# When ScalarE scales an expert's result rows: behind the copy of U3, or behind the silu of C12

## The chip, the core and the metric

The kernel runs on one core of one Trainium2 chip. The metric is device time in microseconds (us). Five engines work side by side, each in its own order: TensorE (PE in the profile; its weight loads are PEld), VectorE (DVE), ScalarE (ACT), GpSimd (POOL), and SyncE (SP), which issues DMAs. An engine's instruction waits on semaphores that other engines raise, and everything queued behind it on that engine waits with it.

## The reference, cut to what matters

The model block is a gated cross-attention followed by a gated mixture of experts. Only the second part is touched. Each of 8 experts takes the 615 tokens with the highest claim on it, runs a two-layer network on them, scales each result row by that token's gate, and adds the row to the token's output:

```python
        xg = x[disp_tok].reshape(E, cap, Dm)
        h = jax.nn.silu(jnp.einsum('ecd,edh->ech', xg, W1) + b1[:, None, :])
        out = jnp.einsum('ech,ehd->ecd', h, W2) + b2[:, None, :]
        gated = out * disp_g.reshape(E, cap, 1)
        y = jnp.zeros((N, Dm), x.dtype).at[disp_tok].add(gated.reshape(E * cap, Dm))
```

E is 8, cap is 615 (held as 616 columns, two halves of CH = 308), Dm is 512, and the hidden width is 2048.

## The kernel before

The attention takes about the first half of the time. After it, the experts run one after another, experts 0 to 7. The order on every engine is the order in which the Python code issues the instructions: both halves stand under `tc.manual_schedule()`, so no planner moves anything.

An expert has an up projection in NP = 8 steps, `up(e, i, hook)` for i = 0 to 7, and then a down projection in two parts, `down(e, m, hook)`. One step of `up` makes two blocks of 128 hidden units for both halves of the columns, by Strassen's scheme in Winograd's form: seven products in place of eight. All are fp32 and go through `product` (L933), four matmuls to a product in the profile. In the order of TensorE they are:

1. `p1`, then `p2` (both `ps<-xg_t,w`). ScalarE copies `p1` out to `p1s` (L961); VectorE adds `p2` to it, which gives `c11` (L964); ScalarE takes the silu of it with bias (L957).
2. A product added onto `p1` (`ps<-tg,s1w`). It may start only when `p1s` has been copied out. ScalarE copies the sum to `u2` (L986). Then the product `p5` (also `ps<-tg,s1w`). VectorE forms V = `p5` + `u2` (L991).
3. A product added onto `p1` (`ps<-xg_t,w`); ScalarE copies it to `u3` (L994). VectorE forms `c22` = `p5` + `u3` (L996), ScalarE its silu.
4. The product `p3` (`ps<-xg_t,s1w`); VectorE forms `c12` = `p3` + V (L1001), ScalarE its silu.
5. A last product added onto `p1` (`ps<-tg,w`); ScalarE takes the silu of it directly: silu 21 (L957).

In between, `up` calls `hook(1)` (behind the silu of `c11`) and `hook(3)` (behind the silu of `c12`). The function behind them, `in_up(i, n)`, puts the side work there:

- At `hook(1)`: on VectorE the four sums `sum_h` of the step before (L914 to L917, through `sums_t`), on GpSimd the four weight sums `sum_w1` of the step after (L645 to L648, through `sums_of`), on SyncE the load of a weight block (L656), and `lay_out(e - 1, i)`. The last takes one tile of 128 columns of the *previous* expert's result `o_t`, transposes it in blocks on VectorE (L866 or L870), and issues four DMAs on SyncE (L874) that bring it into rows, in the tile `eo`.
- At `hook(3)`, for i = 1 to 5: `put_laid(e - 1, i - 1)`. It scales the rows that the step before laid out by their gates, on ScalarE and in place (L893), and then issues the scatter that adds them to the output, an indirect DMA from GpSimd (L1101). Expert 0 has no previous expert, so there are 7 x 5 = 35 scalings of this kind; the last expert's rows go another way, after the loops.
- Also at `hook(3)`: `route_on()`, one piece of the selection of tokens for a later expert. A typical piece is `narrow`: one small matmul that counts (L714), and ten small VectorE instructions (L700 to L732).

GpSimd takes its work in the order issued too: the scatter of a step, then the weight sums that `hook(1)` of the next step asks for. Three `eo` tiles and two `s1w` tiles are in use in turn.

In `down` the products are longer (16 matmuls), ScalarE has little to do, and neither scalings nor scatters of `put_laid` are issued.

## Time and profile before

| What | Value |
|---|---|
| median of 3 runs | 2031.45 us (2030.32 to 2032.4) |
| the profiled execution, its time | 2030.15 us |
| the profiled execution, its span in the trace | 2028.4 us |
| granted TensorE clock, mean over the span | 0.977 |
| busy, share of the span: PE, DVE, ACT, POOL | 95%, 63%, 42%, 30% |
| up steps of expert 1: PE busy in 1173 to 1233 us | 59.16 of 60.00 us |
| L893, the scaling | 35 times, median 706 ns |
| L1101, the scatter from `eo` with `slots` | 35 times, median 1560 ns |

Times in the views run from the span's start. In a timeline each row has the start, the time, the engine, the line, the operation, the tiles, and in square brackets the idle time of the engine before it with what ended it; a row marked x4 holds four instructions in a run. A matmul's record reaches a little past the start of the next one, so the spacing of starts is the better measure of PE's pace than the recorded time. One up step without anything else takes 7.26 us in this trace (from one L994 to the next: 1178.59, then 7.26 and again 7.26 later).

### The profile page before, as it was taken

Reading aid. Unit: us, or ns where it says so; the run is one execution under the profiler, and the core shown is the slowest. Engines: PE = TensorE matmul, PEld = TensorE weight load, DVE = VectorE, ACT = ScalarE, POOL = GpSimd, SP = SyncE. Lnnn points to the kernel's source line nnn. Section 1 sums busy time; section 2 is a strip of 40 time slices with the busy share of each in tenths; the row PEclk is TensorE's granted clock in tenths of the full one; section 3 lists DMA queues with packets and bytes.
Section 4 is the critical chain, followed back from the end, with each engine's and each line's share of the span. In section 5 each row is a group of like instructions: output and inputs, shape, how many; then the busy total and the mean of one; then the engine's idle time right before and its main releaser. Section 6 shows DMA issues by size and latency. Waiting matters only on the chain.

```text
span 2028.4 us, 27201 instructions
## 1 busy us (share of the span) xinstructions
PE 1930.5 (95%) x8784; PEld 1151.1 (57%) x8784; DVE 1279.6 (63%) x2693; ACT 851.8 (42%) x2014; POOL 603.5 (30%) x798
## 2 busy tenths in 40 slices
PE   7989999999999999998669999999999999999997
PEld 3334444444444444444346777777777777777775
DVE  3566666667666666766568675776767667772540
ACT  3656667566666756565213032230403223041321
POOL 1001110010111001110135463536545365464533
PEclk9999999999999999998779999999999999999998
DMA  7243434434343443333511545344553534455332
GB/s 259 74 116 90 128 110 120 125 94 139 104 123 110 121 124 96 103 114 89 150 51 52 157 88 135 89 114 117 110 148 87 138 89 111 124 113 136 88 68 26
DMA packets 291678, 224.58 MB, mean 111 GB/s; under 512 B 26768, under 2 KB 260944, under 8 KB 291536
## 3 DMA queue, kind: packets, MB, share of 16 engines
q1 hardware_dynamic: 282704, 201.96, 35.7%
q0 software_dynamic: 8832, 20.88, 5.6%
q8 instruction: 71, 1.16, 0.3%
q14 instruction: 71, 0.58, 0.1%
HBM read 107.75 MB, written 29.77 MB: 68 GB/s over the span
## 4 chain that ended last, share of the span: by engine, by line
PE 73%; DVE 8%; ACT 7%; DMA 4%; issue 4%; SPq 2%; POOL 1%; POOLq 0%; ACTq 0%; DVEq 0%
PE ps L933 40%; PE pj L300 13%; PE po L423 6%; PE s L352 6%; PE pt L236 5%; ACT by_part L375 3%; DVE nm L361 2%; ACT pr L375 2%; DMA laid_p<-by_part 2%; DVE p_t L405 1%; DMA w<-in_W 1%; SPq L874 1%; SPq L380 1%; DVE ht L917 1%; ACT q_t L309 1%
## 5 line engine op out<-in xcount | busy, mean ns | idle before, releaser
L361 DVE TENSOR_REDUCE nm<-s 128x2 f32<-128x1024 f32 x256 | 298.1, 1204 | 52.6 <-PE s L352 52.5
L395 ACT COPY p_t<-pt 128x512 f32<-128x512 f32 x256 | 138.1, 589 | 276.7 <-PE pt L236 276.5
L933 PE MATMUL ps<-xg_t,w 128*128 128x308 f32 x768 | 220.1, 423 | 0.5 <-ACT u L986 0.5
L223 POOL TENSOR_TENSOR rstd<-rstd,nhalf 128x1 f32<-128x1 f32 x64 | 37.0, 578 | 613.9 <-DVE rstd L222 613.9
L352 PE MATMUL s<-k_t,q_t 32*128 32x512 f32 x1024 | 193.9, 653 | 25.4 <-ACT by_part L375 17.8
L933 PE MATMUL ps<-h,w 128*128 128x308 f32 x768 | 207.5, 425 | 0.0
L375 ACT ACTIVATE by_part<-s,nm 128x512 f32<-128x512 f32 x256 | 174.5, 691 | 53.1 <-DVE nm L361 47.8
L933 PEld LDWEIGHTS ps<-xg_t,w 128*128 128x128 f32 x768 | 145.8, 190 | 53.9 <-ACT u L986 1.0
L375 ACT ACTIVATE pr<-s,nm 128x512 f32<-128x512 f32 x256 | 174.4, 697 | 0.0
L933 PEld LDWEIGHTS ps<-h,w 128*128 128x128 f32 x768 | 143.7, 190 | 52.6 <-issue 3.2
L236 PEld LDWEIGHTS pt<-ident,pr 128*128 128x128 f32 x1024 | 112.5, 143 | 103.4 <-issue 100.3
L405 DVE STREAM_TRANSPOSE p_t<-laid_p 128x512 f32<-128x512 f32 x256 | 165.9, 686 | 5.0 <-DMA laid_p<-by_part 4.7
L933 PE MATMUL ps<-tg,s1w 128*128 128x308 f32 x512 | 145.3, 426 | 9.3 <-ACT p1s L961 5.5
L442 DVE TENSOR_TENSOR o_t<-po,over 128x512 f32<-128x512 f32 x32 | 22.1, 691 | 207.3 <-ACT over L438 207.3
L236 PE MATMUL pt<-ident,pr 128*128 128x128 f32 x1024 | 143.4, 284 | 2.7 <-ACT pr L375 2.7
L423 PE MATMUL po<-p_t,v_s 128*32 128x512 f32 x1024 | 142.4, 628 | 0.9 <-DVE p_t L405 0.9
L933 PE MATMUL ps<-ht,s2w 128*128 128x308 f32 x512 | 137.9, 426 | 0.0
L957 ACT ACTIVATE h<-c,b 128x308 f32<-128x308 f32 x192 | 101.4, 549 | 74.3 <-DVE c L996 72.1
L933 PEld LDWEIGHTS ps<-tg,s1w 128*128 128x128 f32 x512 | 94.9, 190 | 52.8 <-issue 20.5
L300 PE MATMUL pj<-ctx_t,wk 128*128 128x512 f32 x256 | 117.0, 600 | 7.1 <-DMA ctx_t<-in_ctx_t 7.1
L933 PEld LDWEIGHTS ps<-ht,s2w 128*128 128x128 f32 x512 | 95.5, 190 | 34.8 <-issue 1.8
L300 PE MATMUL pj<-xn_t,wq 128*128 128x512 f32 x248 | 111.6, 592 | 0.0
(191 smaller groups left out, 3105.0 us busy)
## 6 DMA issues: line engine op xcount, KB each, us to landing
laid_p<-by_part SPq DMA_DIRECT2D x512, 128.0 KB
w<-in_W SPq DMA_DIRECT2D x128, 256.0 KB
w<-in_W SPq DMA_DIRECT2D x64, 512.0 KB
x<-in_x SPq DMA_DIRECT2D x64, 256.0 KB
laid<-xg SPq DMA_DIRECT2D x140, 64.0 KB
out_x<-x SPq DMA_DIRECT2D x32, 256.0 KB
xn_rows<-xn SPq DMA_DIRECT2D x32, 256.0 KB
ctx_t<-in_ctx_t SPq DMA_DIRECT2D x28, 256.0 KB
```

The lines of the kernel that those rows point to most:

```text
L223: nc.gpsimd.tensor_tensor(rstd, rstd, nhalf, ALU.pow)
L236: nc.tensor.transpose(pt[:, c, :], src[:, c * P : (c + 1) * P], ident)
L300: nc.tensor.matmul(ps, lhsT=lhs(ic), rhs=rhs(ic), start=(ic == 0), stop=(ic == DC - 1))
L352: nc.tensor.matmul(ps[i // 2][:, i % 2, :], lhsT=q_t[b, c][r, cols(qc)], rhs=k_t[b, c][r, :], start=True, stop=True,)
L361: nc.vector.tensor_reduce(nm[:, 2 * i : 2 * i + 2], ps[i], AX.X, ALU.max, negate=True)
L375: nc.scalar.activation(to, of, AF.Exp, bias=nm[:, i : i + 1], accum_out=sums[b, c][:, qc, i : i + 1])
L395: nc.scalar.copy(p_t[b, c][i][:, :, cols(qc)].rearrange("p c (q j) -> p c q j", q=DC), pt.rearrange("p c (j q) -> p c q j", q=DC),)
L405: nc.vector.transpose(p_t[b, c][i][:, :, cols(qc)].rearrange("p c (q j) -> p q c j", q=DC), laid[:, :, i - 2].rearrange("p q (c i) -> p q ...
L423: nc.tensor.matmul(po[i * HD : (i + 1) * HD, :], lhsT=v_s[b][:, kc, h * HD : (h + 1) * HD], rhs=pts[i][:, kc, :], start=(kc == 0), stop=(k ...
L442: nc.vector.tensor_tensor(o_t[b][:, c, :], po, over, ALU.mult)
L933: nc.tensor.matmul(ps, lhsT=lhs[k], rhs=rhs[k], start=(k == 0 and not onto), stop=(k == n - 1), skip_group_check=onto,)
L957: nc.scalar.activation(hh[q, i], src, AF.Silu, bias=b1[:, j : j + 1])
```

## The change

`up` gets one more call, `hook(2)`, behind the copy of `u3` on ScalarE and ahead of the sum `c22`. `in_up` puts `put_laid` there and leaves `route_on` at `hook(3)`. Nothing is added or taken away; on ScalarE the scaling now stands ahead of two silus (of `c22` and of `c12`) that it stood behind.

```diff
@@ up
         product([w[:, k, 1, :] for k in k0], [x[:, k, rhalf] for k in k0], p1)
         u3 = temp("u3")
         nc.scalar.copy(u3, p1)
+        hook(2)
         c22 = temp("c", 3)
         tt(c22, p5, u3, ALU.add)
         silu("22", 1, c22)
@@ in_up
             def in_up(i, n):
-
-                if n == 3:
+                if n == 2:
                     if e and 0 < i <= NST:
                         put_laid(e - 1, i - 1)
+                    return
+
+                if n == 3:
                     if e == 0 or i > 1:
                         route_on()
                     return
```

The order of instructions changes on ScalarE alone. On TensorE, VectorE, GpSimd and SyncE every instruction keeps its place and what it waits for.

## The prediction

> **What bounds the kernel now.** I read the page first, then who PE waited for in the stretch of the expert steps (1173 to 2010 us), then the timelines of PE, ScalarE, VectorE and GpSimd for expert 1.

> The page says that TensorE is busy nearly all the time, so only its idle time can be won:

> ```profile
> span 2028.4 us, 27201 instructions
> PE 1930.5 (95%) x8784; PEld 1151.1 (57%) x8784; DVE 1279.6 (63%) x2693; ACT 851.8 (42%) x2014; POOL 603.5 (30%) x798
> ```

> The waits of PE from 1173 to 2010 us (total in us, times, longest) are few, 21 in all:

> ```profile
> PE ps L933 <- issue: 3.0, 12, 0.3
> PE ps L933 <- ACT p1s L961: 2.6, 7, 0.5
> PE ps L933 <- ACT h L957: 0.8, 2, 0.4
> ```

> 21 is 3 for each of the 7 experts that scale rows. The timeline of PE shows where: at the first product that is added onto p1. The first three rows are a step without a stall, the last three one with:

> ```profile
> 1187.66 2.24 PE L933 MATMUL ps<-xg_t,w 128*128 128x308 f32 x8
> 1189.74 2.24 PE L933 MATMUL ps<-tg,s1w 128*128 128x308 f32 x8
> 1191.81 1.20 PE L933 MATMUL ps<-xg_t,w 128*128 128x308 f32 x4
> ...
> 1195.03 2.24 PE L933 MATMUL ps<-xg_t,w 128*128 128x308 f32 x8
> 1197.56 2.31 PE L933 MATMUL ps<-tg,s1w 128*128 128x308 f32 x8 [0.28 <-issue]
> 1199.70 1.20 PE L933 MATMUL ps<-xg_t,w 128*128 128x308 f32 x4
> ```

> The distance of starts is 2.08 us without a stall and 2.53 with one, and the next distance is 2.14 in place of 2.07: a stall shown as 0.28 costs 0.52 us. In expert 1 the other two (at 1205.35 and 1213.32) cost 0.43 and 0.60. They follow steps i = 2, 3 and 4; no stall follows i = 1 and i = 5, though they scale too.

> What PE waits for is p1s, whatever the label: it starts 0.15 us after p1s ends. The timeline of ScalarE:

> ```profile
> 1193.10 0.41 ACT L994 COPY u<-ps 128x308 f32<-128x308 f32 x1 [1.21 <-PE ps L933]
> 1195.10 0.99 ACT L957 ACTIVATE h<-c,b 128x308 f32<-128x308 f32 x2 [1.58 <-DVE c L996]
> 1196.00 0.71 ACT L893 ACTIVATE eo<-eo,gates 128x512 f32<-128x512 f32 x1
> 1196.61 0.50 ACT L957 ACTIVATE h<-ps,b 128x308 f32<-128x308 f32 x1
> 1197.01 0.40 ACT L961 COPY p1s<-ps 128x308 f32<-128x308 f32 x1
> ```

> ScalarE is idle for 1.58 us until c22 comes, and then runs five instructions without a gap; the scaling is in the middle and holds back silu 21 and p1s by 0.61 us (1196.61 less 1196.00). p1 itself was there at about 1196.2. So these steps turn on a loop: p1s, c11, the sums of VectorE, c22, two silus, the scaling, silu 21, the next p1s. c22 is late because VectorE and GpSimd slow each other: the same sum takes 0.47 us in the step where GpSimd rests and 1.00 beside it:

> ```profile
> 1184.05 0.47 DVE L916 TENSOR_TENSOR h<-h,h 128x308 f32<-128x308 f32 x1
> ...
> 1191.78 1.00 DVE L916 TENSOR_TENSOR h<-h,h 128x308 f32<-128x308 f32 x1
> 1192.40 0.96 POOL L647 TENSOR_TENSOR w<-w 128x256 f32<-128x256 f32 x1
> ...
> 1196.98 1.56 POOL L1101 DMA_INDIRECT out_x<-eo,slots  x1 [2.71 <-DMA eo<-laid]
> ```

> The last row shows GpSimd waiting, until 0.27 us after the scaling's end (1196.71): the wait named is an older DMA, the scaling is what came last.

> **The change, part by part.**

> *The scaling leaves the place ahead of p1s.* Per stalled step ScalarE's chain from c22 to p1s is shorter by 0.61 us. PE's lateness at that product (start distances 2.53, 2.43, 2.60 against 2.08) is 0.45, 0.35 and 0.52: each less than 0.61. So each stall goes. Over 21 stalls: 6.4 us shown, plus 0.24 each that the idle time does not show (0.17 of the overlap of two matmuls, 0.07 at the restart), 5.0 us: 11.4 us. Checked by expert 1: 0.52 + 0.43 + 0.60 = 1.55, times 7 is 10.9; experts 5 and 7 have somewhat longer ones. After that the step goes at PE's own pace, 7.26 us, or 7.37 with one counting matmul.

> *The scaling's new place costs nothing.* It stands behind u3 and would run from 1193.5 to 1194.2, in an idle time of 1.58 us (1.49 and 1.66 in the two steps after, 0.89 at i = 5). At i = 1 the idle time is only 0.55, so the silu of c22 comes 0.06 us later; there p1s waits for PE and nothing is lost. Without this cover the price would be 0.61 x 35 = 21 us, if ScalarE were full; it is not.

> *A wait moves forward with it.* The scaling also waits for the four DMAs that bring the rows in. If they are late, the silus of c22 and c12, silu 21 and p1s are queued behind them, and PE behind p1s. The trace's packets of these DMAs: issued from 1185.56, ended by 1189.33; the next sets ended by 1198.12, 1206.19 and 1214.91. The new places of the scalings that use them are about 1193.5, 1200.9, 1208.3 and 1215.7 at PE's new pace, and VectorE's transposes that start the later sets come earlier as well (below). The margins are 4.2, 2.8, 2.1 us, and over 0.8 us at i = 5 even if the transpose did not move. I put nothing.

> *The scatter and, behind it in GpSimd's order, the weight sums move forward.* The scatter starts 0.28 after the scaling, at 1194.5 in place of 1196.98; the sums (1.04 us later) at 1195.5 in place of 1198.0. No instruction of GpSimd waited for PE there, and the `s1w` tile that the sums write is free once PE has passed p3 (1194.1). The scatter's transfer is far from the next one (7 us). What changes is what the sums meet on VectorE: less of L914 to L917, more of `narrow`. In the first such step the sums would start at 1188.3, where VectorE is idle until c11 at 1190.0: `sum_h` is then slowed only in its first half, and c22 comes about 1 us sooner. This is a gain in slack, not counted in us.

> [...] VectorE's load in a full step, from c11 (1197.44) to the end of `narrow` (1205.07), is 7.63 us. `sum_h` takes 3.57 in it (1197.84 to 1201.41) and 1.68 without GpSimd (1183.15 to 1184.83), so undisturbed the load is 5.74. How much will GpSimd add at the new place? The trace has a row near: in `down`, GpSimd's sums meet `narrow`.

> ```profile
> 1195.56 0.17 DVE L718 TENSOR_TENSOR ahead<-ahead,thr 128x7 int32<-128x7 int32 x1
> 1196.23 0.56 DVE L700 TENSOR_TENSOR mask<-gate,cand 128x224 bf16<-128x224 f32 x1
> ...
> 1260.27 0.65 DVE L718 TENSOR_TENSOR ahead<-ahead,thr 128x7 int32<-128x7 int32 x1
> 1261.64 0.97 DVE L700 TENSOR_TENSOR mask<-gate,cand 128x224 bf16<-128x224 f32 x1
> ```

> With L726 (0.38 for 0.17) `narrow` grows by 1.1 us at most. The part of it that GpSimd would meet from 1195.5 on, L726 and L700, grows by 0.6; then L914 and L915 by 0.8 (their rows beside GpSimd), perhaps L916 by 0.5. Sum 1.4 to 1.9, load 7.1 to 7.6, against PE's 7.37. [...] I take the rows: 1.4 to 1.9. Even 7.63 would slip only 0.26 per step for three steps, 0.8 us, inside the 1 us won in the first.

> *Sum:* 2030.15 for the profiled execution less 11.4 is 2018.75. That execution lies 1.3 us under the median, 2031.45; on the median's scale the forecast is 2020.1.

> **The rivals.**

> *VectorE becomes the bound and keeps part of the stalls.* If GpSimd slows VectorE as before and no slack is won, VectorE's chain from 1190.0 to 1210.5 shortens only by its two idle gaps (0.16 and 0.19), and p1s by these and 0.61: 0.96 us per expert in place of 1.55. Expert 7 has no routing and gains all, about 1.8: 6 x 0.96 + 1.8 = 7.5, time 2023.9. For it: VectorE's full steps are without gaps. Against it: GpSimd's sums start 2.5 us earlier, where c11 to c12 read PSUM or VectorE idles.

> *Nothing measurable.* The stalls are there for another reason, such as p1's own lateness: 2031.5. Against it: p1s starts exactly when silu 21 lets it, and in step i = 1, where c22 was early, the same scaling cost PE nothing.

> [...]

> **How the numbers follow.** All stalls gone, 2018.3 to 2022: 0.70. A part kept, 2022 to 2027.4: 0.16. Within 0.2% (4 us, about what a measurement of this kernel can tell from no change): 0.05. Slower: 0.09. The range, 2018.3 to 2026.0, takes the first and nearly all of the second; its lower end is the full gain and the 1.1 to 1.3 us by which runs lie under the median, plus a little.

> **What would show it right or wrong.** Right: no wait of PE at `ps<-tg,s1w` from 1173 to 2010; L893 right behind L994, 2.5 us ahead of before; GpSimd's wait ahead of L1101 shorter; the first L916 of a scaling step back to 0.5; steps of 7.26 or 7.37 in all. Part kept: PE waits at i = 3 and 4 of experts 1 to 6 with VectorE gapless from L964 to L732. Wrong: an idle time of ScalarE ahead of L893 put down to a DMA, L700 and L718 over 1 us, or p1s still 0.15 us ahead of a late PE.

## The result, and the profile after

The changed kernel takes 2022.64 us (median of 5 runs, 2020.46 to 2024.9) against 2031.45 us (5 runs, 2029.3 to 2032.54); the ratio of all runs is 0.9958 with a 95% interval of 0.9943 to 0.9972. A second series beside the experiments gave 2018.81 us (2016.34 to 2020.05) against 2030.33 us: 0.9936, 0.9918 to 0.9954. So the change saves about 9 to 11.5 us. The profiled execution took 2020.52 us. The page after:

```profile
span 2018.7 us, 27201 instructions
PE 1927.6 (95%) x8784; PEld 1153.8 (57%) x8784; DVE 1269.9 (63%) x2693; ACT 857.5 (42%) x2014; POOL 593.4 (29%) x798
```

PE's busy share shows nothing of it, and its waits show all. From 1173 to 2000 us no wait of PE is listed any more, where 21 were listed before. From 1060 us on there are only these, all in expert 0, which scales no rows:

```profile
PE ps L933 <- ACT p1s L961: 2.8, 2, 2.5
PE cnt_ps L714 <- DVE cnt L708: 1.2, 2, 0.8
```

PE's timeline of the two steps of expert 1 that were shown of before:

```profile
1187.92 2.24 PE L933 MATMUL ps<-xg_t,w 128*128 128x308 f32 x8
1190.00 2.24 PE L933 MATMUL ps<-tg,s1w 128*128 128x308 f32 x8
1192.07 1.20 PE L933 MATMUL ps<-xg_t,w 128*128 128x308 f32 x4
...
1195.29 2.24 PE L933 MATMUL ps<-xg_t,w 128*128 128x308 f32 x8
1197.37 2.24 PE L933 MATMUL ps<-tg,s1w 128*128 128x308 f32 x8
1199.44 1.20 PE L933 MATMUL ps<-xg_t,w 128*128 128x308 f32 x4
```

The second step now has the spacing of the first: 2.08 and 2.07 us, where it was 2.53 and 2.14. ScalarE in that step:

```profile
1193.36 0.42 ACT L994 COPY u<-ps 128x308 f32<-128x308 f32 x1 [1.21 <-PE ps L933]
1193.67 0.72 ACT L893 ACTIVATE eo<-eo,gates 128x512 f32<-128x512 f32 x1
1194.75 0.99 ACT L957 ACTIVATE h<-c,b 128x308 f32<-128x308 f32 x2 [0.36 <-DVE c L997]
1195.65 0.50 ACT L957 ACTIVATE h<-ps,b 128x308 f32<-128x308 f32 x1
1196.58 0.42 ACT L961 COPY p1s<-ps 128x308 f32<-128x308 f32 x1 [0.43 <-PE ps L933]
```

The scaling sits in the idle time behind u3, and the copy p1s waits for PE (0.43 us), no longer PE for it. But VectorE and GpSimd in the same step look less calm than the forecast had them (their timelines, one beneath the other):

```profile
1195.04 0.74 DVE L717 TENSOR_SCALAR ahead<-steps 128x7 int32<-128x7 int32 x1
1195.72 1.27 POOL L645 TENSOR_TENSOR s1w<-w 128x256 f32<-128x256 f32 x1
1195.81 1.22 DVE L718 TENSOR_TENSOR ahead<-ahead,thr 128x7 int32<-128x7 int32 x1
...
1199.30 0.47 DVE L964 TENSOR_TENSOR c<-ps,p1s 128x308 f32<-128x308 f32 x1
1200.58 0.47 DVE L916 TENSOR_TENSOR h<-h,h 128x308 f32<-128x308 f32 x1
```

The sums of h are fast again (L916 at 0.47), because in this step GpSimd's weight sums fall on the routing piece `narrow`; there L718 takes 1.22 us in place of 0.17, and c11 comes 4.0 us behind the step's first product (1199.30 less 1195.29), where it came 2.4 behind it before (1197.44 less 1195.03).

Where the 9.7 us between the two spans lie, by the starts of the copies of u3: the stretch from expert 1's first to expert 7's last went from 772.65 to 762.34 us, 10.3 less. The time ahead of expert 0 is 1.4 less, expert 0 takes 1.65 more, the tail 0.4 more. The last three do not come from where the scaling stands: the code there is the same, and other profiles scatter there too (last section). I call the first the *expert stretch* and use it for the experiments, since it repeats to 0.1 us: a second profile of the changed kernel has 762.31. The stalls account for all of it. Added up over the up steps of experts 1 to 7, PE's starts at the product added onto p1, and at the restart behind it, lie 11.38 us too far apart in the profile of before and 1.07 in that of after; the difference is 10.3.

### The profile page after: what moved, and what is told of

Read it like the earlier page. It is cut to its first block, busy times and chain, and to the rows that moved or that the text cites. A ratio compares the mean times of both kernels' runs of the same rounds, so it can differ in the third digit from the quotient of the medians.

```text
span 2018.7 us, 27201 instructions
## 1 busy us (share of the span) xinstructions
PE 1927.6 (95%) x8784; PEld 1153.8 (57%) x8784; DVE 1269.9 (63%) x2693; ACT 857.5 (42%) x2014; POOL 593.4 (29%) x798
## 4 chain that ended last, share of the span: by engine, by line
PE 78%; DVE 7%; ACT 7%; issue 3%; DMA 3%; SPq 2%; POOL 1%; POOLq 0%; ACTq 0%; DVEq 0%
PE ps L933 45%; PE pj L300 13%; PE po L423 6%; PE s L352 6%; PE pt L236 5%; ACT by_part L375 3%; DVE nm L361 2%; ACT pr L375 2%; DMA laid_p<-by_part 2%; DVE p_t L405 2%; SPq L380 1%; ACT q_t L309 1%; PE pj_o L300 1%; DVE mask L700 1%; PE idle L1138 0%
## 5 line engine op out<-in xcount | busy, mean ns | idle before, releaser
L933 PE MATMUL ps<-xg_t,w 128*128 128x308 f32 x768 | 220.7, 423 | 0.5 <-ACT u L986 0.5
L933 PE MATMUL ps<-h,w 128*128 128x308 f32 x768 | 207.5, 425 | 0.0
L933 PEld LDWEIGHTS ps<-xg_t,w 128*128 128x128 f32 x768 | 146.3, 191 | 54.3 <-ACT u L986 1.0
L933 PEld LDWEIGHTS ps<-h,w 128*128 128x128 f32 x768 | 143.7, 190 | 52.6 <-issue 3.2
L933 PE MATMUL ps<-tg,s1w 128*128 128x308 f32 x512 | 145.3, 427 | 3.1 <-ACT p1s L961 2.8
L933 PE MATMUL ps<-ht,s2w 128*128 128x308 f32 x512 | 137.9, 426 | 0.0
L957 ACT ACTIVATE h<-c,b 128x308 f32<-128x308 f32 x192 | 102.3, 550 | 49.1 <-DVE c L997 39.1
L933 PEld LDWEIGHTS ps<-tg,s1w 128*128 128x128 f32 x512 | 96.6, 190 | 41.6 <-issue 5.6
L933 PEld LDWEIGHTS ps<-ht,s2w 128*128 128x128 f32 x512 | 95.5, 190 | 34.8 <-issue 1.8
L352 PEld LDWEIGHTS s<-k_t,q_t 32*128 32x128 f32 x1024 | 53.3, 186 | 102.8 <-ACT pr L375 43.7
```

What stands on the lines that cost most here:

```text
L352: nc.tensor.matmul(ps[i // 2][:, i % 2, :], lhsT=q_t[b, c][r, cols(qc)], rhs=k_t[b, c][r, :], start=True, stop=True,)
L933: nc.tensor.matmul(ps, lhsT=lhs[k], rhs=rhs[k], start=(k == 0 and not onto), stop=(k == n - 1), skip_group_check=onto,)
L957: nc.scalar.activation(hh[q, i], src, AF.Silu, bias=b1[:, j : j + 1])
```

## The experiments

Two explanations were open. A: it is enough that the scaling leaves the place ahead of p1s on ScalarE. B: that alone leaves VectorE as the bound, and what also counts is that GpSimd's scatter and weight sums start earlier and meet other work on VectorE.

**The changed kernel again** (e1). No edit.

> The changed kernel once more, beside the others on one chip. Both theories: 2020 to 2025 us, 6 to 11 us under the kernel before; PE's waits at ps<-tg,s1w in experts 1 to 7 under 0.7 us in total (6.4 before). Where the time lies in this band is open: the profile of the changed kernel had a half-clock window of TensorE of 3.4 us at expert 0's last step, which the profile of before did not have, so runs should differ by steps of about 1.7 us.

Measured: 2018.81 us, 1.2 us under the range I had given; expert stretch 762.3. PE's only listed wait in experts 1 to 7 is one of 0.2 us, as expected.

**The scaling moved, GpSimd held back** (e2).

```diff
@@ in_up, against the changed kernel
                 if n == 2:
                     if e and 0 < i <= NST:
-                        put_laid(e - 1, i - 1)
+                        scale_laid(e - 1, i - 1)      # L893 alone
                     return
                 if n == 3:
+                    if e and 0 < i <= NST:
+                        # GpSimd copies h["12", i][:, 0:1], then the scatter
+                        put_laid(e - 1, i - 1, h[e]["12", i])
```

> The scaling at its new place on ScalarE, but GpSimd held as it was: the scatter is issued at the old place, behind a read by GpSimd of one column of the silu of C12, so that scatter and weight sums start near their old times. Theory A (the 0.61 us that the scaling took between c22 and p1s is enough by itself): PE's waits at ps<-tg,s1w in experts 1 to 7 under 1.5 us, time within 2 us of the changed kernel. Theory B (VectorE is then the bound; the earlier weight sums of GpSimd were needed too): about 0.6 us of loss stays per expert 1 to 6, 3 to 4 us in all, mostly behind steps 3 and 4, and the time is 3 to 4 us above the changed kernel.

Measured: 2025.11 us (2022.78 to 2032.82), ratio to the kernel before 0.997 (0.9957 to 0.9983); expert stretch 767.3. PE's waits in experts 1 to 7, and ScalarE and PE around steps 2 and 4 of expert 1:

```profile
PE ps L939 <- ACT p1s L967: 2.9, 9, 0.5
...
1203.16 0.99 ACT L963 ACTIVATE h<-c,b 128x308 f32<-128x308 f32 x2 [1.03 <-DVE c L1003]
1204.46 0.40 ACT L967 COPY p1s<-ps 128x308 f32<-128x308 f32 x1
...
1219.00 0.99 ACT L963 ACTIVATE h<-c,b 128x308 f32<-128x308 f32 x2 [1.68 <-DVE c L1003]
1220.30 0.40 ACT L967 COPY p1s<-ps 128x308 f32<-128x308 f32 x1
1220.84 2.31 PE L939 MATMUL ps<-tg,s1w 128*128 128x308 f32 x8 [0.39 <-ACT p1s L967]
```

The first of the three stalls is gone. Then c22 comes later from step to step (ScalarE waits 1.03, then 1.68 us for it), and although no scaling stands in the chain, p1s is late and PE stalls. B is right, and by more than I had put on it: the time is 6.3 us above the changed kernel's, where I had 3 to 4.

**The read by itself** (e5), the control to e2.

```diff
@@ put_laid, against the kernel before
         nc.scalar.activation(eo[:m, :], eo[:m, :], AF.Copy, scale=gates[e][:m, s : s + 1])
+        seen = ex.tile([P, 1], F32, tag="seen", name="seen", bufs=2)
+        nc.gpsimd.tensor_copy(seen, behind_h[:, 0:1])     # h[e]["12", i]
```

> The control of e2_scatter_back: the scaling at its old place, and GpSimd's read of the silu of C12 ahead of the scatter. It isolates what the read itself costs, so that the distance to e2 is the scaling's place on ScalarE alone, with GpSimd at about the same times. If the read is harmless: the stretch from expert 1's first copy of u3 to expert 7's last within 1 us of the kernel before (772.7 us in its profile), 21 stalls. If the read itself is what kept part of the loss in e2: that stretch 2 us or more longer than before.

Measured: 2034.81 us against 2031.25, ratio 1.0019 (1.001 to 1.0028); expert stretch 775.8, so 3.1 longer than before. PE's waits in experts 1 to 7, all at the same product under three labels, are still 21, now up to 0.9 us each:

```profile
PE ps L935 <- ACT p1s L963: 8.1, 17, 0.9
PE ps L935 <- issue: 0.9, 3, 0.3
PE ps L935 <- ACT h L959: 0.4, 1, 0.4
```

The read is not harmless: GpSimd's weight sums start 0.2 to 0.3 us later behind u3 than before (means of each step over experts 1 to 7), and the loop pays for it. So e2 must be compared with e5: 775.8 less 767.3, 8.5 us, is about what the scaling's place on ScalarE is worth with GpSimd late. GpSimd does not run at the very same times in both: in e2 the scatter starts 0.1 to 0.2 us earlier behind u3 in steps 1 and 2, and 0.2 to 0.6 us later in steps 3 to 5. The remaining 6.1 us, down to the 761.2 of a loop without stalls (e3, next), are what a late GpSimd costs, the read included.

**The weight sums early, the scaling at its old place** (e3).

```diff
@@ in_up, against the kernel before
                 if n == 3:
                     if e and 0 < i <= NST:
+                        if i + 2 < NP:
+                            sum_w1(e, i + 2)
                         put_laid(e - 1, i - 1)
...
-                if 0 < i < NP - 1:
+                if 0 < i < NP - 1 and not (e and 1 < i <= NST + 1):
                     sum_w1(e, i + 1)
```

> The scaling at its old place (behind the silu of C12), but the weight sums that the next step asks for are issued on GpSimd one hook earlier, ahead of the scatter, so that they start when p3 has passed and meet less of the sums of h. Theory A in its narrow form (only the scaling's place counts): 21 stalls stay, 6 us of waits shown, time as before (2031). The loop theory (p1s, c11, sums, c22, silus, scaling, silu 21, p1s is a loop a little longer than PE's step, and any 0.5 us taken out of it frees PE): c22 comes up to 1 us sooner, most stalls vanish, 2021 to 2026.

Measured: 2017.47 us (2015.12 to 2022.52), ratio 0.9932 (0.9912 to 0.9951), faster than either theory had it; expert stretch 761.2 us, 11.4 less than before. No wait of PE is listed in experts 1 to 7. Its rows of GpSimd, ScalarE and PE in step 2 of expert 1:

```profile
1194.89 0.72 POOL L645 TENSOR_TENSOR s1w<-w 128x256 f32<-128x256 f32 x1 [2.56 <-PE cnt_ps L714]
1195.80 0.71 ACT L893 ACTIVATE eo<-eo,gates 128x512 f32<-128x512 f32 x1
1197.07 0.42 ACT L961 COPY p1s<-ps 128x308 f32<-128x308 f32 x1 [0.16 <-PE ps L933]
1197.85 2.24 PE L933 MATMUL ps<-tg,s1w 128*128 128x308 f32 x8
```

The scaling stands where it stood, between the silus and p1s, and p1s still waits for PE. The scaling's new place is thus not needed for the gain, if the weight sums are early. They start here 1.04 us behind u3, where the changed kernel has them at 2.3 to 2.4 and the kernel before at 4.0 to 5.1. The loop theory holds, A in its narrow form does not.

**The scaling one place further ahead** (e4, and again as e9).

```diff
@@ in_up, against the changed kernel
                 if n == 2:
-                    if e and 0 < i <= NST:
-                        put_laid(e - 1, i - 1)
                     return
...
                 if e == E - 1 and i == NP - 1:
                     in_order(e)
+                if e and 0 < i <= NST:
+                    put_laid(e - 1, i - 1)
```

> The scaling one place further ahead, behind the silu of c11 (hook 1) instead of behind u3. Theory A (there is idle time for it there too): within 2 us of the changed kernel. Rival (the wait moves forward with it: the rows of a step land too late): at i = 4 and 5, where the changed kernel's margin is 0.8 to 2.1 us, ScalarE waits for the DMAs ahead of L893, u3 is late, and PE waits for u3 at ps<-tg,w; 0.5 to 1 us in 7 to 14 places, 4 to 12 us above the changed kernel.

> e4_behind_11 again, beside e8 on one chip: 2017 to 2020 us by its last median, 761.3 us from expert 1's first copy of u3 to expert 7's last.

Measured: 2018.79 us (0.9938, 0.9921 to 0.9956) and 2020.47 us (0.995, 0.9937 to 0.9964); expert stretch 761.2 us in both, again without a wait of PE in experts 1 to 7. The e9 median lies 0.5 us above the range I had given it. GpSimd starts earlier still here: the weight sums 1.0 us behind u3. The rows of the previous expert land just in time even there: of the scaling's 102 waits on semaphores six take more than 38 ns, and the longest 290 ns (minimum, median and maximum in e4):

```profile
L893 ACTq EVENT_SEMAPHORE  x102: 17/38/290, 1180.2 to 1919.8; - x102
```

**One piece of routing fewer in expert 0** (e6 from the changed kernel; e7 together with e4).

```diff
-                if e == 0 and i in (2, 4, 6):
+                if e == 0 and i in (2, 4):
                     route_on()
```

> The changed kernel with one piece of routing fewer in expert 0's up steps (the extra route_on of step 6 is dropped; the pieces follow later, in down). All profiles so far have a wait of PE of some 2.5 us and one of 0.5 us there, and most a half-clock window right behind. If that wait comes from VectorE's load by routing: it shrinks, the half-clock window goes with it, 2 to 5 us under the changed kernel. If it comes from the sums of W2 on GpSimd alone: no change, or the wait moves to down.

> e4_behind_11 and e6_one_less together: the scaling behind the silu of C11, and one piece of routing fewer in expert 0. If both gains are real and independent: no wait of PE in experts 1 to 7 (761.3 us from expert 1's first u3 to expert 7's last) and none of 2.5 us in expert 0; 3 to 6 us under the changed kernel, about 2014 to 2016 us. If the routing pieces that are pushed back make later experts' steps stall: no gain over the changed kernel.

Measured: 2029.15 us (0.9984, 0.9974 to 0.9994) and 2027.79 us (0.9983, 0.9975 to 0.999): most of the gain lost, where I had expected 2 to 6 us less than the changed kernel. The wait in up goes, and a larger one comes in expert 0's down (e7):

```profile
1158.33 1.09 DVE L853 STREAM_TRANSPOSE xg_t<-laid 128x512 f32<-128x512 f32 x1 [9.45 <-DMA laid<-xg]
...
1163.03 0.17 PE L714 MATMUL cnt_ps<-cnt,all_p 128*128 128x7 bf16 x1 [7.78 <-DVE cnt L708]
```

The gather for expert 1 is one hook later; VectorE waits 9.45 us for its rows, with the next routing piece queued behind, and PE waits for that piece's counting. The wait moved to down, as one of the expectations had it, but by way of the gather and not of the sums of W2.

**The piece moved instead of dropped** (e8, with e4).

```diff
-                if e == 0 and i in (2, 4, 6):
+                if e == 0 and i in (2, 3, 4):
                     route_on()
```

> e4_behind_11 with the third extra piece of expert 0's routing moved from step 6 to step 3 (in e7 it was dropped there, the gather for expert 1 came one hook later, and PE lost 7.8 us in down behind a transpose that waited for its rows). Now the gather keeps its time. If the wait of 2.5 us in expert 0 comes from the piece in step 6 beside the sums of W2: it is gone, down stays as in e4, and the time is 3 to 5 us under e4 (half of it the half-clock window behind the wait). If VectorE is simply full in expert 0's steps: the wait comes back at steps 4 or 5, no gain over e4.

Measured: 2015.35 us (2011.68 to 2024.45) against 2030.77 before, ratio 0.9935 (0.9914 to 0.9957), the lowest median of all; expert stretch 761.2. PE's waits from 1060 to 1990 us:

```profile
PE cnt_ps L714 <- DVE cnt L708: 0.8, 1, 0.8
PE ps L933 <- POOL s1w L648: 0.6, 1, 0.6
PE ps L933 <- ACT p1s L961: 0.5, 1, 0.5
```

The 2.5 us are gone. The time from expert 0's first copy of u3 to expert 1's is 122.0 us, against 125.5 in the changed kernel and 123.8 before. In time alone the intervals of e8, e3, e4, e9 and e1 overlap; what sets e8 apart is seen in its profile.

## Why the prediction was right, and where not

*Which wait, and its size: right.* I had 21 stalls of PE at the product added onto p1, worth 11.4 us with what the idle times do not show. e3, e4 and e8, where all are gone, have an expert stretch of 761.2 us, 11.4 under 772.65. The changed kernel gets 10.3 of it: PE is still late at three such products (at 1330.9, 1687.4 and 1799.0; the starts are 0.12, 0.31 and 0.24 us too far apart, and at each restart 0.07 more), too little to be listed as waits.

*The scaling's new place costs nothing: right.* It lies in idle time, and L893 has no listed wait for the rows. e4 shows that even the place before has room.

*The scatter and the sums start 2.5 us earlier: right* (1194.68 and 1195.72; I had 1194.5 and 1195.5).

*"So each stall goes": the step that was too simple.* I compared 0.61 us with each stall as it stood. But a stall that is removed brings PE forward, and VectorE then has less time up to the next: in e2 the later stalls came back. In steps 3 and 4 (means of experts 1 to 6) c22 starts 2.00 and 2.04 us behind u3 in e2, but 1.54 and 1.45 in the changed kernel, about as before (1.46 and 1.62). So the change did not make c22 earlier there; the earlier weight sums kept it from falling back, and I had put them down as slack "not counted in us". That slack was smaller than I said: in step 2 c22 came 0.6 us sooner (1.50, now 0.90), not 1. It was enough, so the size of the gain came out right partly by luck. With GpSimd late, ScalarE's part is 8.5 us (e5 to e2); with GpSimd early, the scaling's place is worth nothing (e3). The two gains are not a sum: both shorten the same loop, and PE's own pace caps them. My first rival had this mechanism; the changed kernel escaped it because it does both at once.

*VectorE's load at the new place: right in the mean, under-sized in one step.* I took from `down` that `narrow` would grow by at most 1.1 us, and 1.4 to 1.9 with the sums of h. In expert 1's step 2 `narrow` took 4.33 us (1195.04 to 1199.37) against 1.90 before (1195.38 to 1197.28): 2.4 more. L718 ended there only as GpSimd's L645 ended (1197.03 and 1196.99), but not in the next step: it took 0.63 us and ended at 1203.96, while L645, which had started first, ran on to 1204.52. Of the 48 L718 from 1173 us on, three took 1.22 us and none of the others over 0.65.

From c11 to the end of `narrow`, steps 2, 3 and 4 of expert 1 took 9.11, 6.41 and 7.34 us, 7.6 in the mean. I had 7.1 to 7.6. The same three spans were 7.28, 7.63 and 7.78 before, so VectorE has no less to do; GpSimd now disturbs it behind c22 more than ahead of it. c11, which reads PSUM, takes a median of 0.48 us beside GpSimd's weight sums (21 times before, 35 after, at most 0.48) and without them. The 1.6 us by which c11 came later were made up directly behind it: the sums of h took 1.75 us (1199.69 to 1201.44) in place of 3.57, and ScalarE's wait for u3 shrank from 1.21 to 0.38 us. I had named L700 and L718 over 1 us as a sign that the forecast was wrong. L718 got there (L700 stayed at 0.97), and PE did not lose: it was the wrong sign to name, since the slack decides and not the one instruction.

*The time.* I gave 2020.1; the two series have 2022.64 and 2018.81. The stretch I forecast repeats to 0.1 us, while the runs of one series differ by 4 us and more for a reason outside it, which follows; that the first median lies 2.5 us above the forecast and the second 1.3 below says little.

## What to carry to other kernels

Where engines form a loop that is a little longer than the bound engine's step, look at every member of the loop. Here 0.6 us off ScalarE alone won part of the stalls (e2), earlier weight sums alone won all of them (e3), and once the loop was shorter than the step a further gain in it was worth nothing (761.2 us in e3, e4 and e8 alike). Before a stall is counted as gone, ask what is late once the bound engine comes earlier. A moved instruction also moves what waits for it on other queues; here the weight sums behind the scatter decided as much as the scaling itself, and a read of one column on GpSimd cost 3 us.

## What the hardware showed that I had not expected

Behind the same wait in expert 0 (2.46 us before, 2.45 after) PE went on at full clock in the profile of before, and at half clock for 3.4 us in that of after: its matmuls there start 0.51 us apart in place of 0.26. The busy times by stretch, first of after, then of before (the mean granted clock stands behind POOL's: 0.66 and 1.00):

```profile
1105.00:1110.00 5.00, 4.67 (x12) 3.20 (x13) 3.18 (x9) 1.05 (x3) 0.00 (x0) 0.66 0.00 0
...
1106.00:1112.00 6.00, 5.25 (x21) 3.88 (x22) 4.78 (x16) 2.74 (x7) 0.00 (x0) 1.00 0.00 0
```

The attention and the change to the experts hold more such intervals, and their number differs from run to run. Ahead of expert 0's first u3 they last 65 us in the profile where it comes earliest (1049.5 us, e4) and 92 us in the two where it comes latest (1061.1 and 1061.5, e2 and e6): half of the 27 us is about the 12 us between them. By this estimate it is the main reason why runs of one kernel spread by 4 us and more. The granted clock of the runs fits it: over the 59 of the kernel before beside e5, time and mean granted clock have a correlation of -0.82; the shortest (2026.93 us) had a clock of 0.981, the longest (2039.29 us) one of 0.974. An estimate from these, the share of clock not granted times the span, gives 14.5 us more lost in the longest, which took 12.4 us more.
